# Final norms behind the next block's sets, the last two tiles in two banks, and first biases in three operations

## The chip, the cores and the metric

The kernel runs on one core of a Trainium2 chip. The metric is the device time of one execution in microseconds (us). The time before is 3287.83 us, the median of three runs (3287.54 to 3289.83).

The engines are named as in the profile: PE (matrix products; PEld is its weight load), DVE (vector), ACT (scalar, activations and copies), POOL (the general engine, used here for small per-row values and some subtractions) and SP, whose queue issues all DMAs in program order. Each engine works through its own queue in order; a waiting instruction holds everything behind it.

## What is computed

An attention stage over windows of 128 rows, then a feed-forward stage whose weights are mixed from eight experts for each of the four batches; after each stage a layer norm and a residual. Cut to what matters:

```python
x = x + _layernorm(_L0_attn_ref(_layernorm(x), w_qkv))       # 4 x 2048 x 512
h = relu(x @ gate_w1.T + gate_b1); g = mean over rows (h @ gate_w2.T + gate_b2)
mW1 = W1 + sum_e g[e] * TW1[e];  mb1 = b1 + g @ Tb1
mW2 = W2 + sum_e g[e] * TW2[e];  mb2 = b2 + g @ Tb2
u = gelu(x @ mW1.T + mb1)                                    # 2048 wide
x = x + _layernorm(u @ mW2.T + mb2)
```

All in float32. The last line's layer norm and sum are the "final norms" below. `mb1` are the "first biases".

## The kernel before

**Two phases.** The attention phase runs over 256 slots (64 windows of four groups); next to the scores, exponentials, transposes and values, it carries the projections, the gate's products and, from slot 84, the mixer. The mixer is a generator (`mixer`, steps called with `next(blend)`): each step loads an expert's tile of 512 KB three steps ahead (L119) and adds one on DVE (L144, 128x1024); after eight of them a ninth step makes sums (L152 to L155) and stores the mixed weights to DRAM. The order of instructions is written out by hand; the program doesn't reorder.

**First biases.** When a batch's gate is done, `gate_end` gives four functions. `experts` brings g into SBUF; `first_biases` (L216) adds the eight experts' biases to b1, one SCALAR_TENSOR_TENSOR for each expert (L219), every one on the result of the one before. It is called once per batch: three times in the attention phase, and for the last batch in the feed-forward phase, behind product 5 of block 0.

**The feed-forward phase** runs over 16 blocks of 512 rows (K = 0 to 15; four per batch). A block has two halves.

The first half is four sets (c = 0, 2, 4, 6). Each set makes seven products by a Winograd-like scheme on 256x256 quarters. `begin(n)` issues X (A11), a copy of X into bank Y on ACT (L851), Z (S1) and a copy of it (L853). `middle(n, ...)` issues Y (A12), X (S2), a copy cpb of X (L865), then `end` of the set before (product A22 into that set's X, six gelus on ACT, and `more_sums`: two subtractions on POOL, L889 and L890), two gelus of its own, Z (S4), the add cpb on DVE (L871), X (S3) and the add cpv on DVE (L874). Between them stand steps of the mixer, four per set in most blocks, two per set in block 0 and in the last block of a batch. The first set of a block has no `end` in it; the last set's `end` is issued inside product 0 of the second half (`closing`), after the first four of sixteen products.

The second half (`second`) is seven products of 256 columns (L912, `product2`), each followed by adds into the tiles y0 (tiles 0 and 1 of 128 rows) and y1 (tiles 2 and 3) on DVE (L931). Its weights come through three buffers, `load_second` loading three products ahead. Product 5 completes y1, product 6 completes y0.

**The final norm of a tile** has these parts: `stats` (L85: statistics and aggregate on DVE, then the sum with EPS, L92, and the power, L94, on POOL), `standard` (L987: the shift on POOL, L990, then scale and shift on ACT in place, L991), and `finish` (L993: the residual tile x1 plus y on DVE, L996, and the store, L997). `load_x1` (L983) loads a residual tile from DRAM; the tag "x1" has two buffers, so a third load waits until the first one's store has left.

In a block the order is: tiles 2 and 3 in product 6 (`stats`, `standard`, then the add of c21, then `finish`); `stats` of tiles 0 and 1; their residuals are loaded; the two wait in the list `pending`. In sets 0 and 1 of the next block one each is taken: `standard` behind `begin`, `finish` behind `middle`. For the last block they come at the end of the program.

Of the kernel before, what the change touches and what calls it, by code (L numbers as in the profile page):

```python
# [9 lines left out]
F32 = mybir.dt.float32  # L10
AF = mybir.ActivationFunctionType
ALU = mybir.AluOpType
AX = mybir.AxisListType
# [3 lines left out]
P = 128  # L17
# [9 lines left out]
NX = 8  # L27
# [7 lines left out]
def sandwich(ctx: ExitStack, tc: tile.TileContext, x, w_qkv, gw1, gb1, gw2, gb2, w1, b1, w2, b2, tw1, tb1, tw2, tb2, out):  # L35
# [159 lines left out]
    def gate_end(b, hsum, bank, spare):  # L195

        hm = small.tile([P, KC], F32, tag="hm", name=f"hm_{b}")
        parts = small.tile([P, KC, NX], F32, tag="parts", bufs=1, name=f"parts_{b}")
        part = small.tile([P, NX], F32, tag="part", bufs=1, name=f"part_{b}")
        gc = small.tile([NX, 1], F32, tag="gc", name=f"gc_{b}")  # L200

        def means():

            nc.vector.tensor_reduce(hm, hsum, AX.X, ALU.add)
            nc.vector.tensor_tensor(parts, gw2_sb, hm.unsqueeze(2).to_broadcast([P, KC, NX]), ALU.mult)
            nc.vector.tensor_reduce(part, parts.rearrange("p k e -> p e k"), AX.X, ALU.add)

        def experts():
            pg = bank(f"pg_{b}")
            nc.tensor.matmul(pg[:, :NX], lhsT=ones, rhs=part, start=True, stop=True)  # L210
            nc.tensor.matmul(pg[:NX, NX : NX + 1], lhsT=part, rhs=ones[:, :1], start=True, stop=True)
            nc.vector.scalar_tensor_tensor(gc, pg[:NX, NX : NX + 1], 1.0 / L, gb2_col, ALU.mult, ALU.add)
            nc.vector.scalar_tensor_tensor(g_all[b], pg[:, :NX], 1.0 / L, gb2_row, ALU.mult, ALU.add)
            nc.vector.tensor_copy(gcb[:NX, :], gc.to_broadcast([NX, P]))

        def first_biases():  # L216
            mb1 = mb1_all[b]
            for e in range(NX):
                nc.vector.scalar_tensor_tensor(  # L219
                    mb1, tb1_sb[:, e, :], g_all[b][:, e : e + 1], b1_sb if e == 0 else mb1, ALU.mult, ALU.add  # L220
                )

        def second_biases():
            pb = bank(f"pb_{b}")
            nc.tensor.matmul(pb, lhsT=gcb, rhs=tb2_sb, start=True, stop=True)
            mb2 = spare(f"mb2s_{b}")
            nc.vector.tensor_copy(mb2, pb)
            nc.sync.dma_start(mb2_d[b], mb2)

        return means, experts, first_biases, second_biases  # L230
# [563 lines left out]
    with ExitStack() as fctx:  # L794
# [107 lines left out]
                w2s[g] = wts.tile([P, HC, Q], F32, tag="w2s", bufs=3, name=f"w2s_{g}")  # L902
                nc.sync.dma_start(w2s[g], m2_d[K // NBLK][:, order[j]])

        def product2(K, j, bank, right, start, closing=None):

            w = w2s.pop(7 * K + j)
            for c in range(HC):
                if c == 2 and closing:
                    end(*closing)  # L910
                for t in range(2):
                    nc.tensor.matmul(  # L912
                        bank[:, t, :],
                        lhsT=right(c - c % 2)[:, c % 2, ts(t, P)],
                        rhs=w[:, c, :],
                        start=(start and c == t == 0),
                        stop=True,
                        skip_group_check=True,
                    )
            load_second(7 * K + j + 3)  # L920
# [4 lines left out]
        def second(K, closing, steps, load_x1):  # L925

            mb = mb2_of[K // NBLK]
            mlo, mhi = (mb[:, i * Q : (i + 1) * Q].unsqueeze(1).to_broadcast([P, 2, Q]) for i in range(2))
            y = {h: io.tile([P, 2, D], F32, tag=f"y{h}", bufs=1, name=f"y{h}_{K}") for h in range(2)}
            (c11, c21), (c12, c22) = ((y[h][:, :, :Q], y[h][:, :, Q:]) for h in range(2))  # L930
            add = lambda out, bank, other: nc.vector.tensor_tensor(out, bank, other, ALU.add)  # L931
            b11 = lambda c: us[c][:, :, :Q]
            t3 = lambda c: us[c][:, :, Q:]
            b21 = lambda c: us[c + HC][:, :, :Q]
            b22 = lambda c: us[c + HC][:, :, Q:]
            t1 = lambda c: t1s[c]
            X, Z, Y = bank2("x2", f"px2_{K}"), bank2("z2", f"pz2_{K}"), bank2("y2", f"py2_{K}")

            product2(K, 0, X, b11, True, closing)
            steps()  # L940
            add(c11, X, mlo)
            yield
            product2(K, 1, Z, t1, True)
            steps()
            add(c22, Z, mhi)
            yield
            product2(K, 2, Y, b21, True)
            for c in range(0, HC, 2):
                nc.gpsimd.tensor_tensor(t1s[c], b22(c), t1s[c], ALU.subtract)
            steps()  # L950
            add(c11, Y, c11)
            yield
            product2(K, 3, X, t1, False)
            for c in range(0, HC, 2):
                nc.gpsimd.tensor_tensor(b21(c), b21(c), t1s[c], ALU.subtract)
            steps()
            add(c12, X, mlo)
            yield
            product2(K, 4, Z, b22, False)
            steps()  # L960
            add(c12, Z, c12)
            load_x1(K, 2)
            load_x1(K, 3)
            yield
            product2(K, 5, X, t3, False)
            steps()
            add(c21, X, mhi)
            add(c22, X, c22)
            yield
            Y = bank2("y2", f"py2b_{K}")  # L970
            product2(K, 6, Y, b21, True)
            for t in range(2):
                standard(K, t + 2, y[1][:, t, :], stats(y[1][:, t, :], f"d{K}_{t + 2}"))
            steps()
            add(c21, Y, c21)
            for t in range(2):
                finish(K, t + 2, y[1][:, t, :])
            for t in range(2):
                pending.append((K, t, y[0][:, t, :], stats(y[0][:, t, :], f"d{K}_{t}")))
                load_x1(K, t)  # L980
            yield

        def load_x1(K, t):  # L983
            x1s[K, t] = io.tile([P, D], F32, tag="x1", name=f"fx1_{K}_{t}")
            nc.sync.dma_start(x1s[K, t], x1_d[K * WB + t])

        def standard(K, t, y, sm):  # L987
            mv, rs = sm
            shift = small.tile([P, 1], F32, tag="shift", name=f"shift_{K}_{t}")
            nc.gpsimd.tensor_scalar(shift, mv[:, 0:1], rs, -1.0, ALU.mult, ALU.mult)  # L990
            nc.scalar.activation(y, y, AF.Identity, bias=shift, scale=rs)  # L991
# [57 lines left out]
        nc.sync.dma_start(win[last]["x"], x[NB - 1, L - P :])  # L1049
        for g in range(3):  # L1050
            load_second(g)
        pending = []

        def mixing(*counts):

# [8 lines left out]
        for K in range(NBK):  # L1064
            b, k = divmod(K, NBLK)
            if k == 0:
                mb2_of[b] = io.tile([P, D], F32, tag="mb2", bufs=1, name=f"mb2_{b}")
                nc.sync.dma_start(mb2_of[b], mb2_d[b])
            before = None
            for c in range(0, HC, 2):  # L1070
                n = K * (HC // 2) + c // 2
                if n == 0:

                    for cc in (0, HC):
                        for f in range(2):
                            bias = mb1_all[0][:, cc + f : cc + f + 1]
                            nc.scalar.activation(us[cc][:, f, :], us[cc][:, f, :], AF.Gelu_apprx_tanh, bias=bias)
                    more_sums(0, 0)
                    for f in hooks[("set", 0)]:
                        f()  # L1080
                    continue
                S = begin(n)
                if pending:
                    standard(*pending[0])

                if n < 2:
                    step = mixing(0, 0, 0, 0)
                elif K == 0 or (k == NBLK - 1 and b + 1 < NB):
                    step = mixing(0, 1, 0, 1)
                else:  # L1090
                    step = mixing(1, 1, 1, 1)
                middle(n, S, before, step)
                before = (n, S)
                if pending:
                    finish(*pending.pop(0)[:3])
                for f in hooks.get(("set", n), ()):
                    f()
            for j, _ in enumerate(second(K, before, mixing(2, 2, 2, 2, 2, 2, 1), load_x1)):

                if j == (0 if K else 3) and K + 1 < NBK:  # L1100
                    load_block(K + 1)
                if j == (2 if K else 5) and K + 1 < NBK:
                    right_sums(K + 1)
                for f in hooks.get(("product", K, j), ()):
                    f()
        for p in pending:
            standard(*p)
            finish(*p[:3])


# [54 lines left out]
```

## Time and profile before

| | us |
|---|---|
| median of three runs (lowest, highest) | 3287.83 (3287.54, 3289.83) |
| the profiled execution | 3289.09 |
| its span, first to last instruction | 3287.3 |
| PE busy (share of the span) | 3257.1 (99%) |
| DVE busy | 2072.9 (63%) |
| ACT busy | 1573.1 (48%) |
| POOL busy | 720.8 (22%) |
| mean granted clock of PE, share of full speed | 0.996 |

The profile is of one execution. Its span is what the timeline shows; the execution's own time is 1.8 us longer. The attention phase ends at about 1722 us of the span, the feed-forward phase fills the rest; the last matmul ends at 3276.57.

"Idle before, <- releaser" in a line is the time in which the engine stood before that instruction, and the instruction that released it. In the chain of waits each line is a piece of the work that ended last, followed back from the end. Idle time of an engine other than PE costs nothing unless PE waits for it in turn.

### The profile page before, as it was taken

The page shows a single profiled execution, that of the slowest core. Times are in us where ns is not written, and L with a number is a line of the kernel's source. Part 1 is how long each engine was busy: PE and PEld are TensorE (multiplying, and loading weights), DVE is VectorE, ACT ScalarE, POOL GpSimd, SP SyncE. Part 2 cuts the span into 40 slices and gives each one's busy share as a digit, 9 for nine tenths or more (in the row PEclk, how much of TensorE's full clock was granted, in tenths as well). Part 3 has the DMA queues.
Part 4 walks back from the last instruction along what each step waited for, and adds up shares of the span by engine and source line. Part 5 has one row for each costly group of instructions (what it writes and reads, how often), then busy time and mean ns, then how long its engine had stood idle before and what let it go on. Part 6 is the DMA issues. An engine that isn't in the chain of part 4 may idle for free.

```text
span 3287.3 us, 58445 instructions
## 1 busy us (share of the span) xinstructions
PE 3257.1 (99%) x22830; PEld 2624.7 (80%) x22830; DVE 2072.9 (63%) x2887; ACT 1573.1 (48%) x4212; POOL 720.8 (22%) x841
## 2 busy tenths in 40 slices
PE   9999999999999999999999999999999999999998
PEld 7777777777777777777768888888888888888887
DVE  5656555888888888888884665565556656412221
ACT  3777767777776777767772221212222122222121
POOL 1111110122221122111113322332322333321222
PEclk9999999999999999999999999999999999999999
DMA  2111111556665566656777788988788888732332
GB/s 85 49 59 53 43 52 53 169 193 203 215 211 184 193 201 215 195 178 198 237 255 270 266 293 324 327 294 296 274 322 323 302 288 305 278 107 90 128 128 77
DMA packets 316118, 651.96 MB, mean 198 GB/s; under 512 B 22969, under 2 KB 89657, under 8 KB 295490
## 3 DMA queue, kind: packets, MB, share of 16 engines
q1 hardware_dynamic: 315842, 648.22, 56.9%
q8 instruction: 180, 2.95, 0.4%
q14 instruction: 96, 0.79, 0.1%
HBM read 538.03 MB, written 110.10 MB: 197 GB/s over the span
## 4 chain that ended last, share of the span: by engine, by line
PE 95%; DVE 1%; DMA 1%; ACT 1%; POOL 1%; issue 0%; SPq 0%; DVEq 0%; POOLq 0%; ACTq 0%
PE pm L443 18%; PE px L814 13%; PE ptp L547 10%; PE px L912 9%; PE sc L510 7%; PE pz L912 7%; PE pz L814 6%; PE pmg L163 6%; PE po L563 6%; PE py L912 3%; PE py L814 3%; PE py2b L912 3%; DMA exps<-in_tw 1%; PE pto L240 1%; PE ptx L269 1%; PE pt_a L363 1%
## 5 line engine op out<-in xcount | busy, mean ns | idle before, releaser
L144 DVE SCALAR_TENSOR_TENSOR acc<-exps,g,acc 128x1024 f32<-128x1024 f32 x512 | 685.2, 1338 | 183.0 <-DMA exps<-in_tw 176.7
L532 ACT ACTIVATE pr<-sc,nm 128x384 f32<-128x384 f32 (+1 forms) x1024 | 574.9, 582 | 211.2 <-DVE nm L519 211.1
L519 DVE TENSOR_REDUCE nm<-sc 128x2 f32<-128x768 f32 (+1 forms) x512 | 449.6, 918 | 281.8 <-PE sc L510 280.0
L549 ACT COPY prT<-ptp 128x512 f32<-128x512 f32 x736 | 385.8, 593 | 165.9 <-PE ptp L547 160.9
L991 ACT ACTIVATE y<-y,shift,rs_d 128x512 f32<-128x512 f32 x64 | 52.0, 813 | 739.1 <-POOL shift L990 739.1
L547 PEld LDWEIGHTS ptp<-ident,pr 128*128 128x128 f32 x2944 | 330.0, 141 | 54.5 <-issue 33.8
L547 PE MATMUL ptp<-ident,pr 128*128 128x128 f32 x2944 | 372.8, 276 | 0.0
L814 PE MATMUL px<-tT,w 128*128 128x256 f32 x1512 | 349.9, 379 | 1.9 <-ACT cpb L865 1.9
L814 PEld LDWEIGHTS px<-tT,w 128*128 128x128 f32 x1512 | 286.7, 190 | 42.3 <-ACT cpb L865 3.3
L510 PE MATMUL sc<-k,q 32*128 32x384 f32 (+2 forms) x2816 | 243.5, 423 | 5.6 <-ACT pr L532 5.4
L871 DVE TENSOR_TENSOR cpb<-pz,cpb 128x512 f32<-128x512 f32 x63 | 43.5, 690 | 325.0 <-PE pz L814 278.2
L92 POOL TENSOR_SCALAR ve_b<-mv_b 128x1 f32<-128x1 f32 x64 | 47.1, 736 | 841.5 <-DVE mv_b L90 841.5
L912 PE MATMUL px<-w2s,u 128*128 128x256 f32 x1024 | 228.9, 379 | 0.7 <-ACT last L274 0.7
L532 ACT ACTIVATION_READ_ACCUMULATOR pr<-sc,nm 128x1 f32 x1024 | 224.0, 219 | 0.0
L912 PEld LDWEIGHTS px<-w2s,u 128*128 128x128 f32 x1024 | 194.5, 190 | 27.3 <-ACT last L274 0.9
L163 PE MATMUL pmg<-gT,gw_sb 128*128 128x512 f32 x480 | 215.9, 592 | 0.0
L563 PE MATMUL po<-prT,v 128*32 128x128 f32 x5888 | 214.6, 277 | 0.1
L563 PEld LDWEIGHTS po<-prT,v 128*32 128x32 f32 x5888 | 145.2, 109 | 71.7 <-issue 56.8
L889 POOL TENSOR_TENSOR t<-u 128x512 f32<-128x512 f32 x64 | 84.0, 1313 | 504.6 <-ACT u L826 488.8
L443 PE MATMUL pm<-xnT,wqkv 128*128 128x256 f32 x744 | 183.8, 390 | 0.0
L443 PEld LDWEIGHTS pm<-xnT,wqkv 128*128 128x128 f32 x744 | 135.1, 191 | 41.6 <-ACT oT L570 22.7
L510 PEld LDWEIGHTS sc<-k,q 32*128 32x128 f32 x2816 | 119.1, 184 | 61.2 <-issue 45.9
(168 smaller groups left out, 5301.4 us busy)
## 6 DMA issues: line engine op xcount, KB each, us to landing
exps<-in_tw SPq DMA_DIRECT2D x512, 512.0 KB, 5.8
w2s<-m2d SPq DMA_DIRECT2D x112, 1024.0 KB, 6.1
acc<-in_w SPq DMA_DIRECT2D x64, 512.0 KB, 6.4
x<-in_x SPq DMA_DIRECT2D x64, 256.0 KB, 3.0
m1d<-acc SPq DMA_DIRECT2D x64, 256.0 KB, 6.0
m2d<-acc SPq DMA_DIRECT2D x64, 256.0 KB, 6.6
w<-m1d SPq DMA_DIRECT2D x16, 1024.0 KB, 8.0
fxT<-xTd SPq DMA_DIRECT2D x16, 1024.0 KB, 8.7
```

The source lines that it names most:

```text
L144: nc.vector.scalar_tensor_tensor(acc, ets.pop(n), g_all[b][:, e : e + 1], acc, ALU.mult, ALU.add)
L163: nc.tensor.matmul(pm, lhsT=gw1_sb[:, kc, ts(oc, P)], rhs=xT[:, kc, :], start=(kc == 0), stop=(kc == KC - 1))
L443: nc.tensor.matmul(bank[key][:, half, :], lhsT=a[:, kc, ts(half, P)], rhs=b[:, kc, :], start=(begins and half == kc == 0), stop=True, skip ...
L510: nc.tensor.matmul(scs[r // 2][:, r % 2, col : col + nj * W], lhsT=q[rows, g, ts(W_ % WB, W)], rhs=k_of[kb][rows, g, j0 * W : (j0 + nj) * ...
L519: nc.vector.tensor_reduce(st["nm"][:, h : h + 2], scs[u][:, :, : nk * W], AX.X, ALU.max, negate=True)
L532: nc.scalar.activation(pr[:, : nk * W], scs[r // 2][:, r % 2, : nk * W], AF.Exp, bias=st["nm"][:, h : h + 1], accum_out=st["den"][:, h : h ...
L547: nc.tensor.transpose(pt[:, r, :], st["pr"][g * 4 + r][:, ts(j, W)], ident)
L549: nc.scalar.copy(prT, pt)
L563: nc.tensor.matmul(po[r * E : (r + 1) * E, 0, :], lhsT=v_of[kb][:, jj, h * E : (h + 1) * E], rhs=prT[:, r, :], start=(j == 0), stop=(j == ...
L814: nc.tensor.matmul(bank[:, f, :], lhsT=factor[:, f, kc * P : (kc + 1) * P], rhs=right[:, kc, :], start=(start and f == 0 and kc == 0), sto ...
L889: nc.gpsimd.tensor_tensor(t1s[c], b12, us[c][:, :, :Q], ALU.subtract)
L912: nc.tensor.matmul(bank[:, t, :], lhsT=right(c - c % 2)[:, c % 2, ts(t, P)], rhs=w[:, c, :], start=(start and c == t == 0), stop=True, ski ...
```

## The change

Three parts.

1. `first_biases`: one product of all eight experts' biases with g (128x128), one sum over the experts (128x128 to 128x16), and one add of b1.
2. In all blocks but the last, tiles 2 and 3 join the list `pending` in product 6 instead of being finished there, and tiles 0 and 1 follow. Behind each set of the next block, first the tiles normed behind the set before are finished (`normed_y`), then, if these were tiles 2 and 3, the residuals of tiles 0 and 1 are loaded, then up to two more tiles get their `standard`. So tiles 2 and 3 are normed behind set 0 and finished behind set 1; tiles 0 and 1 are normed behind set 1 and finished behind set 2.
3. In the last block the residuals of tiles 0 and 1 are loaded after product 4 into buffers of the tag "cp". Product 6 runs tile by tile: tile 0 into bank y2, tile 1 into bank z2. Statistics of the finished half of each tile are taken ahead; then each tile is added, its second half measured, both halves aggregated, normalised on DVE (`normalize`, L97) and finished on its own.

```diff
         def first_biases():
             mb1 = mb1_all[b]
-            for e in range(NX):
-                nc.vector.scalar_tensor_tensor(
-                    mb1, tb1_sb[:, e, :], g_all[b][:, e : e + 1], b1_sb if e == 0 else mb1, ALU.mult, ALU.add
-                )
+            weighted = small.tile([P, NX, FC], F32, tag="weighted", bufs=1, name=f"weighted_{b}")
+            nc.vector.tensor_tensor(weighted, tb1_sb, g_all[b].unsqueeze(2).to_broadcast([P, NX, FC]), ALU.mult)
+            nc.vector.tensor_reduce(mb1, weighted.rearrange("p e c -> p c e"), AX.X, ALU.add)
+            nc.vector.tensor_tensor(mb1, mb1, b1_sb, ALU.add)
...
-        def product2(K, j, bank, right, start, closing=None):
-            w = w2s.pop(7 * K + j)
+        def product2(K, j, bank, right, start, closing=None, tiles=range(2)):
+            w = w2s[7 * K + j]
             for c in range(HC):
                 if c == 2 and closing:
                     end(*closing)
-                for t in range(2):
+                for t in tiles:
...
             load_x1(K, 2)
             load_x1(K, 3)
+            if K + 1 == NBK:
+                for t in range(2):
+                    load_x1(K, t, "cp", 4)
...
             Y = bank2("y2", f"py2b_{K}")
-            product2(K, 6, Y, b21, True)
+            if K + 1 < NBK:
+                product2(K, 6, Y, b21, True)
+                for t in range(2):
+                    pending.append((K, t + 2, y[1][:, t, :], stats(y[1][:, t, :], f"d{K}_{t + 2}")))
+                steps()
+                add(c21, Y, c21)
+                for t in range(2):
+                    pending.append((K, t, y[0][:, t, :], stats(y[0][:, t, :], f"d{K}_{t}")))
+                yield
+                return
+
+            Z = bank2("z2", f"pz2b_{K}")
+            product2(K, 6, Y, b21, True, tiles=(0,))
+            product2(K, 6, Z, b21, True, tiles=(1,))
             for t in range(2):
                 standard(K, t + 2, y[1][:, t, :], stats(y[1][:, t, :], f"d{K}_{t + 2}"))
-            steps()
-            add(c21, Y, c21)
+            halves = [small.tile([P, 2, 6], F32, tag="halves", bufs=2, name=f"halves_{t}") for t in range(2)]
+            for t in range(2):
+                nc.vector.bn_stats(halves[t][:, 0, :], c11[:, t])
+            def summed(t, bank):
+                nc.vector.tensor_tensor(c21[:, t], bank[:, t, :], c21[:, t], ALU.add)
+                nc.vector.bn_stats(halves[t][:, 1, :], c21[:, t])
+                mv = small.tile([P, 2], F32, tag="mv", name=f"mv_e{t}")
+                nc.vector.bn_aggr(mv, halves[t])
+                rs = small.tile([P, 1], F32, tag="rs", name=f"rs_e{t}")
+                nc.gpsimd.tensor_scalar(rs, mv[:, 1:2], EPS, None, ALU.add)
+                nc.gpsimd.tensor_tensor(rs, rs, mhalf, ALU.pow)
+                return mv, rs
+
+            sm = summed(0, Y)
             for t in range(2):
                 finish(K, t + 2, y[1][:, t, :])
-            for t in range(2):
-                pending.append((K, t, y[0][:, t, :], stats(y[0][:, t, :], f"d{K}_{t}")))
-                load_x1(K, t)
+            normalize(y[0][:, 0, :], y[0][:, 0, :], sm)
+            sm = summed(1, Z)
+            finish(K, 0, y[0][:, 0, :])
+            normalize(y[0][:, 1, :], y[0][:, 1, :], sm)
+            finish(K, 1, y[0][:, 1, :])
...
                 S = begin(n)
-                if pending:
-                    standard(*pending[0])
...
                 middle(n, S, before, step)
                 before = (n, S)
-                if pending:
-                    finish(*pending.pop(0)[:3])
+
+                for p in normed_y:
+                    finish(*p)
+                for p in normed_y:
+                    if p[1] >= 2:
+                        load_x1(p[0], p[1] - 2)
+                normed_y.clear()
+                for p in pending[:2]:
+                    standard(*p)
+                    normed_y.append(p[:3])
+                del pending[:2]
...
-        for p in pending:
-            standard(*p)
-            finish(*p[:3])
```

## The prediction, as it was put on record

> **What bounds the kernel now.** First the page's share of busy time, then what TensorE (PE) waited for, then the places of those waits in order of time, last the chain that ends the span.
>
> ```profile
> PE 3257.1 (99%) x22830; PEld 2624.7 (80%) x22830; DVE 2072.9 (63%) x2887; ACT 1573.1 (48%) x4212; POOL 720.8 (22%) x841
> ```
>
> PE is the bound: 30.2 us of 3287.3 are without a matmul. The change leaves every matmul in place (the two-bank form issues the same 32 records), so it can win only from these 30 us. The waits of PE (total, times, longest):
>
> ```profile
> PE pm L443 <- DVE q L461: 4.8, 3, 2.5
> PE py L814 <- ACT py L851: 3.8, 3, 2.3
> PE px L814 <- ACT cpb L865: 1.9, 3, 1.1
> ```
>
> The last two rows lie behind three of the 15 block ends (blocks 0, 3 and 7): stalls of 2.26 and 1.06, 0.56 and 0.41, 0.98 and 0.42 us, together 5.69. One of them in the timeline (start, duration, engine, line; in brackets the idle time before and what ended it):
>
> ```profile
> 2114.32 1.89 PE L814 MATMUL pz<-tT,w 128*128 128x256 f32 x8
> ...
> 2115.43 0.81 ACT L991 ACTIVATE y<-y,shift,rs_d 128x512 f32<-128x512 f32 x1 [0.89 <-POOL shift L990]
> 2116.15 0.58 ACT L851 COPY py<-px 128x512 f32<-128x512 f32 x1
> 2116.78 1.99 PE L814 MATMUL py<-fxT,w 128*128 128x256 f32 x8 [0.56 <-ACT py L851]
> ...
> 2122.64 1.99 PE L814 MATMUL px<-tT,w 128*128 128x256 f32 x8 [0.41 <-ACT cpb L865]
> ```
>
> The reader is to see the order on ACT: the norm of tile 3 (L991) sits ahead of the copy py that PE needs, and waits for its shift. The second stall is the same with tile 0's norm ahead of the copy cpb (ACT had waited 4.07 us for that shift). At the other 12 block ends the same waits fit into PE's slack.
>
> In the attention phase two DVE-bound stalls stand behind the first biases (timeline of DVE, then of PE):
>
> ```profile
> 1011.02 0.20 DVE L219 SCALAR_TENSOR_TENSOR mb<-tb_sb,g,b_sb 128x16 f32<-128x16 f32 x1
> 1011.26 1.86 DVE L219 SCALAR_TENSOR_TENSOR mb<-tb_sb,g,mb 128x16 f32<-128x16 f32 x7
> 1013.03 0.54 DVE L99 TENSOR_SCALAR x<-x,mv_c,rs_c 128x512 f32<-128x512 f32 x1
> ```
> ```profile
> 1018.47 1.99 PE L443 MATMUL pm<-xnT,wsum 128*128 128x256 f32 x8 [2.11 <-DVE q L461]
> ```
>
> From 1010.20 to 1018.42 DVE has no gap, and PE's operands (scores, pm) were ready by 1014.9. The same queue ends in a 2.50 us stall at 1437.8. The first-bias groups at 591 and 1816 have none behind them that they cause: at 591 DVE is idle 1.77 us soon after; at 1816 the stall belongs to ACT.
>
> The end of the chain (start, length, what):
>
> ```profile
> 3269.65 6.92 PE py2b L912 x32
> ...
> 3277.20 0.69 DVE fx L996
> 3277.89 0.02 issue
> 3277.91 2.06 DMA out<-fx
> 3279.97 0.02 issue
> 3279.99 2.75 DMA fx<-x1d
> ```
>
> After the last matmul (3276.57) 10.73 us pass: the residual of tiles 0 and 1 is loaded only when the stores of tiles 2 and 3 have left their buffers, and only then added.
>
> **Part 1: norms of a block moved behind the next block's sets.** At the end of a block ACT loses the norms of tiles 2 and 3, and the two others no longer stand ahead of cpb. ACT is then idle when X (A11) is complete, copies at once, and the six stalls go: -5.69 us. Where do the norms land? A set lasts 7 products of 1.73 us = 12.1, the first 6 = 10.4. In set 0 they follow the two gelus behind cpb: cpb at 6.9 after the set's start, gelus to 8.4, two norms at 0.81 to 10.0, while the next copy py is due at 12.1. Without ACT's and the adds' delays the last statistics end at 1823.8 at the latest block end (block 0, set start 1817.4), 2 us ahead of the norms. Cost nothing; the cover is 2.1 us. In set 1 the shifts of tiles 0 and 1 queue on POOL behind the two subtractions of set 0 (L889, L890, median 1.27 each). Measured from the next copy py these start at -5.5; undisturbed they end at -2.9, the shift at -2.6, two norms at -1.0: nothing. PE starts the product that needs the copy at +1.47, the copy takes 0.57, so ACT may be 0.9 late before PE waits.
>
> DVE: the same four adds (0.68 each), now two behind set 1 and two behind set 2 instead of two in product 6 and one in each of sets 0 and 1; four steps of the mixer (1.28), two adds (0.69) and these fill 7.9 of 12.1 us.
>
> SP: four stores and two loads per block move. The two loads wait until the stores have landed, and hold the mixer's loads queued behind them:
>
> ```profile
> 2309.01 0.95 SPq L997 DMA_DIRECT2D out<-fx  x2
> 2317.59 0.97 SPq L985 DMA_DIRECT2D fx<-x1d  x2
> 2318.61 1.45 SPq L119 DMA_DIRECT2D exps<-in_tw  x3
> ```
> ```profile
> 2323.75 1.28 DVE L144 SCALAR_TENSOR_TENSOR acc<-exps,g,acc 128x1024 f32<-128x1024 f32 x1 [4.85 <-DMA exps<-in_tw]
> ```
>
> Today that pause of 9.60 us from store to next expert load, plus 5.14 until the weights are there, hits set 1. After the change it starts about 2.9 us into set 2; three prefetched tiles are used, and the fourth step waits. With pause + landing = S, DVE has worked off that step, two adds, two steps, the cpb add, a step and the cpv add (7.9 us) at 2.9 + S - 12.1 + 7.9 = S - 1.3 after the start of set 3. The closing product A22 (in product 0 of the second half) needs cpv at 12.1 + 1.73 = 13.8. So PE waits from S = 15.1. The block shown has 14.7; with the mean wait for a store (84.8 us over 32, two per block: 5.3), issues of 1.6 and the median landing of 6.9 in this phase, S is 13.8. Value taken: 0.5 us in all over the eight blocks with four steps per set (blocks 1, 2, 4, 5, 6, 8, 9, 10); bounds 0 and, at the longest store wait of the profile (8.5, pause 10.5) and the longest landing (11.8), 8 x 7.2 = 58.
>
> **Part 2: last two tiles one by one.** Tile 0's bank is complete 3.46 us before the last matmul, at 3273.11. DVE until then: adds to 3270.98, statistics of tiles 2 and 3 to 3272.85, two half statistics. A 128x256 BATCH_NORM_STATS is not in the trace: between 0.18 (six elements) and 0.69 (512); I take 0.42, since an add goes from 0.69 to 0.43 at half size. So DVE reaches tile 0's add at 3273.6 and its mean and variance at 3274.7. The adds of tiles 2 and 3 follow their norms (ACT ends 3274.17 and 3275.50) to 3276.2, tile 0's normalisation (L99's kind, 0.53) to 3276.7. Then tile 1: add 0.43 to 3277.05, half statistics from 3277.1, and by today's spacing at 3278.40 (aggregate 0.1 behind the end, POOL 0.27 after it starts, pow 0.31 later for 0.57) the scale is there 1.57 us after the half statistics start: 3278.7. Normalise 0.53, add 0.68: 3280.0. Today the last add ends at 3284.21 and the span at 3287.3, so 3.1 follow: 3283.1. The residuals are loaded some 14 us ahead into free cp buffers. Gain 4.15 us; three ops of half size, each off by up to 0.27, make it 3.3 to 4.9.
>
> **Part 3: first biases.** Eight dependent operations take 2.01 us (1011.02 to 1013.03). New: a 128x128 product, between 0.19 (128x32, L205) and 0.43 (128x256), by size 0.29; a reduction of 128 elements, between 0.21 (32, L206) and 0.92 (768, L519), by size 0.30; an add of 16, 0.14 to 0.19, taken 0.18; with 0.02 between them 0.83. Saved 1.18 (0.41 to 1.41) per group, and it counts at the two stalls, since everything behind was ready: -2.36 us (-0.8 to -2.8). The groups at 591 and 1816 save nothing.
>
> **Sum.** -5.69 - 4.15 - 2.36 + 0.5 = -11.7 us. The profiled execution took 3289.09 us, its span 3287.3 and 1.8 around it; it lies 1.26 above the median of the runs shown, 3287.83. From the median: 3276.1 us.
>
> **Rivals.** *The clock adds to the gain.* Right behind the 2.50 us stall the granted clock is 0.50 from 1440.7 to 1444.1; behind the 2.11 us stall it is not. If the shorter stall (1.3 us) no longer trips it, 3.4 us at half speed give back 1.7: 3274.4. Against it: the clock halves at 1642.1 too, behind stalls of 0.7 us at most.
> The Trainium skill (TensorE: Matmul & The Clock Gate, "What's actually happening") says the gate watches free-running windows of about 3.4 us and halves after an idle one. The 3.4 us length agrees with the trace; that one is needed idle doesn't, since 2.5 us did it. By its rule no stall here would cost clock, and 3276.1 stands.
>
> *ACT waits for POOL in set 1.* For it: L889 and L890 stretch to 1.79 and 2.14 us, a shift to 1.10, when DVE runs the mixer. All at once: subtractions to -1.5, shifts to +0.7, norms to +1.5, copy to +2.1 where 1.45 is the limit: 0.65 in each of 15 blocks, +9.8: 3285.9. Against: at that point of set 1 DVE no longer catches up, so it mostly adds out of PSUM.
> The Trainium skill (GPSIMD Engine Reference, "1. Specifications") says GpSimd shares its SBUF interfaces with VectorE and meets contention from instructions with two SBUF inputs. The mixer step has two, and 2.14 against 1.27 agrees; where they always met, this rival's time would follow.
>
> *DVE takes ACT's place.* The stalls come after a late DVE (at 2104 and 2108 it waited 3.12 and 2.60 us for expert weights); if its adds then hold PE at the same block ends, the 5.69 return: 3281.8. Against: nothing PE needs in the next set's first 8 us comes from DVE but tT, ready 3 us early at 1816.0.
>
> *SP's pause, the other side.* S above 17.4 in the eight blocks makes 8 x 2.3 = 18.7 us and the kernel slower by over 0.2%; at S = 18.5, 8 x 3.4 = 27: 3303. For: store waits of 8.5 and landings of 11.8 occur. Against: the store there queued behind a 1 MB w2s load, which set 2 doesn't have.
>
> **Chances.** 0.2% (6.6 us) is about what a measurement of this kernel tells from no change: faster means below 3281.25. Forecast 0.60, clock 0.14, POOL 0.08, DVE 0.11, SP 0.07. Faster 0.74, same 0.19, slower 0.07. Range 3273 to 3283: the clock case with the biases' upper bound below, the DVE case with a short tail gain above, 0.85 of the chances; those left out are POOL and SP.
>
> **What would show it.** Right: no waits of PE on ACT's py or cpb at block ends; stalls near 0.9 and 1.3 us at 1016 and 1437; 6.6 us from last matmul to the end. Wrong: ACT idle for POOL's shift in set 1 with PE behind it, or PE's A22 of set 3 waiting for cpv on DVE.

## The result, and the profile after

The changed kernel takes 3272.25 us in the median of six runs (3270.06 to 3274.05); the kernel before, beside it, 3288.83 (3285.61 to 3290.95). The ratio is 0.9951, 95% interval 0.994 to 0.9961: about 16.6 us or 0.5% faster. The forecast was 11.7 us; the measured time lies 0.75 us below the stated range. The profiled execution took 3270.06 us, its span is 3268.3, so in the two profiles the spans differ by 19.0.

| | before | after |
|---|---|---|
| span of the profiled execution, us | 3287.3 | 3268.3 |
| block-end waits of PE on py and cpb, us | 5.7 | none |
| attention stalls, us | 2.11 and 2.50 | 0.88 and 1.27 |
| last matmul to the end, us | 10.7 | 6.8 |
| mean granted clock | 0.996 | 0.999 |

Page of the changed kernel, shares of busy time:

```profile
PE 3249.4 (99%) x22830; PEld 2620.8 (80%) x22830; DVE 2062.9 (63%) x2872; ACT 1569.7 (48%) x4210; POOL 718.9 (22%) x839
```

PE has the same 22830 records and is busy 7.7 us less. Waiting was not all that went: the same matmuls took less time, which points to the clock. What PE still waits for (total, times, longest):

```profile
PE sc L510 <- ACT pr L532: 5.9, 14, 1.0
PE pm L443 <- DVE q L461: 2.3, 3, 1.3
```

The rows with py and cpb are gone, and the longest wait for q is halved. The end of block 3 and the sets behind it, in order of time (start, duration, engine, line):

```profile
2102.70 1.89 PE L814 MATMUL pz<-tT,w 128*128 128x256 f32 x8
...
2102.96 0.57 ACT L851 COPY py<-px 128x512 f32<-128x512 f32 x1 [47.56 <-PE px L814]
...
2104.43 1.89 PE L814 MATMUL py<-fxT,w 128*128 128x256 f32 x8
...
2108.08 0.58 ACT L865 COPY cpb<-px 128x512 f32<-128x512 f32 x1 [2.87 <-PE px L814]
...
2109.29 1.52 ACT L1021 ACTIVATE y<-y,shift,rs_d 128x512 f32<-128x512 f32 x2
```

ACT has idled 47.56 us when PE releases it, and copies at once; PE goes from Z to Y with no gap. The two norms (L1021) come behind the gelus and end at 2110.8, 2.5 us ahead of the next copy.

The first biases of batch 1 on DVE:

```profile
1007.30 0.26 DVE L219 TENSOR_TENSOR weighted<-tb_sb,g 128x128 f32<-128x128 f32 x1
1007.60 0.37 DVE L220 TENSOR_REDUCE mb<-weighted 128x16 f32<-128x128 f32 x1
1008.00 0.18 DVE L221 TENSOR_TENSOR mb<-mb,b_sb 128x16 f32<-128x16 f32 x1
1008.09 0.54 DVE L99 TENSOR_SCALAR x<-x,mv_c,rs_c 128x512 f32<-128x512 f32 x1
```

From the first to the next operation behind them 0.79 us, where the eight took 2.01.

The end. The last matmul is over at 3261.46:

```profile
3261.50 0.42 DVE L994 TENSOR_TENSOR y<-pz2b,y 128x256 f32<-128x256 f32 x1
3261.95 0.43 DVE L995 BATCH_NORM_STATS2 halves<-y 128x6 f32<-128x256 f32 x1
3262.41 0.21 DVE L997 BATCH_NORM_AGGREGATE mv_e<-halves 128x2 f32<-128x12 f32 x1
3262.54 0.64 DVE L1026 TENSOR_TENSOR fx<-fx,y 128x512 f32<-128x512 f32 x1
3262.71 0.54 POOL L999 TENSOR_SCALAR rs_e<-mv_e 128x1 f32<-128x1 f32 x1 [1.89 <-DVE mv_e L997]
3263.34 0.57 POOL L1000 TENSOR_TENSOR rs_e<-rs_e,mhalf 128x1 f32<-128x1 f32 x1
3263.94 0.55 DVE L99 TENSOR_SCALAR y<-y,mv_e,rs_e 128x512 f32<-128x512 f32 x1 [0.77 <-POOL rs_e L1000]
3264.52 0.69 DVE L1026 TENSOR_TENSOR fx<-fx,y 128x512 f32<-128x512 f32 x1
```

No load of a residual lies in this chain any more. The one row that differs from the working is L999: 0.54 us, against 0.23 for the same step before, while DVE adds tile 0's residual; that is why 6.8 us remain and not 6.6.

**Where the 19.0 us of the two spans lie.** The order and number of matmuls are the same, so the n-th matmul of one profile can be set against the n-th of the other; the difference of their start times grows at a few places only:

```
stretch of the kernel before            after minus before, us
0 to 160     (clock halved before, full after)     -3.9
160 to 1010                                        +0.2
the stall at 1016                                  -1.2
the stall at 1437                                  -2.9   (1.2 stall, 1.7 clock)
ends of blocks 0, 3, 7               -3.8, -1.5, -1.9     (-7.3 together)
last matmul to the end                             -3.9
```

The block ends gave 7.3 us and not the 5.7 that the six gaps show. One gap shows why. Before, the eight products of pz started at 2114.32 and those of py at 2116.78: 2.46 us. After, 2102.70 to 2104.43: 1.73. The difference is 0.73 for a gap shown as 0.56, since the gap starts at the modelled end of a matmul and the next one normally starts 0.16 before it. The first group after the gap also took 0.1 longer to start the one behind it. About 0.27 us more per stall, 1.6 for six.

The rest is the clock. Of the stretches where it was halved in the kernel before (near 55, 143, 1441 and 1642 us) one was left, the last. The first two lie in code that the change doesn't touch, the third behind the shortened stall. That third place, before and then after (stretch in us, its length, busy time of PE, PEld, DVE, ACT and POOL with their instructions, then PE's granted clock, DMA share and GB/s):

```profile
1440.72:1444.13 3.41, 3.41 (x16) 2.30 (x18) 2.80 (x4) 1.95 (x6) 0.00 (x0) 0.50 0.71 217
```
```profile
1434.30:1438.00 3.70, 3.70 (x42) 2.47 (x43) 3.50 (x5) 2.48 (x8) 0.00 (x0) 1.00 0.77 252
```

Whether that is chance is what the experiments had to tell.

### The profile page after: what moved, and what is told of

Read it like the earlier page. It is cut to its first block, busy times and chain, and to the rows that moved or that the text cites. A ratio compares the mean times of both kernels' runs of the same rounds, so it can differ in the third digit from the quotient of the medians.

```text
span 3268.3 us, 58364 instructions
## 1 busy us (share of the span) xinstructions
PE 3249.4 (99%) x22830; PEld 2620.8 (80%) x22830; DVE 2062.9 (63%) x2872; ACT 1569.7 (48%) x4210; POOL 718.9 (22%) x839
## 4 chain that ended last, share of the span: by engine, by line
PE 97%; DVE 1%; ACT 1%; issue 0%; DMA 0%; POOL 0%; POOLq 0%; SPq 0%; ACTq 0%; DVEq 0%
PE pm L443 18%; PE px L814 13%; PE px L912 10%; PE ptp L547 10%; PE pz L912 7%; PE pz L814 7%; PE sc L510 7%; PE pmg L163 6%; PE po L563 6%; PE py L912 3%; PE py L814 3%; PE py2b L912 3%; PE pto L240 1%; PE ptx L269 1%; PE pt_a L363 1%; ACT pr L532 1%
## 5 line engine op out<-in xcount | busy, mean ns | idle before, releaser
L851 ACT COPY py<-px 128x512 f32<-128x512 f32 x63 | 35.9, 570 | 803.7 <-PE px L814 803.7
```

## The experiments

All differences below are medians against the kernel before on the same chip, with the ratio's 95% interval. First each part by itself, and the kernel before against itself.

**The norms alone**

```diff
+            if K + 1 < NBK:
+                product2(K, 6, Y, b21, True)
+                for t in range(2):
+                    pending.append((K, t + 2, y[1][:, t, :], stats(y[1][:, t, :], f"d{K}_{t + 2}")))
...
-                if pending:
-                    standard(*pending[0])
...
+                for p in pending[:2]:
+                    standard(*p)
+                    normed_y.append(p[:3])
```

> Part 1 alone: the norms of blocks 0 to 14 behind the next block's sets; first biases and the last block's end as before. Theory (stalls): the six block-end stalls go, 5.7 us off, so about 5.7 below the kernel before; in the profile no wait of PE on ACT's py or cpb, the two attention stalls stay at 2.1 and 2.5 us, the end from last matmul stays 10.7. Rival (the surplus of 4.5 us comes from the clock behind the block-end stalls): about 10 below, and the profile of a kernel with these stalls would show halved clock behind them. Rival (the surplus is chance in where the clock halves): 5.7 below in the median, and the profile's span after taking off half of each halved stretch is 5.7 below the one of before taken likewise.

Measured: 3281.41, 7.2 below before (0.9965 to 0.9985). Its waits of PE have no row of py or cpb; the first two are:

```profile
PE sc L510 <- ACT pr L532: 5.2, 13, 1.0
PE pm L443 <- DVE q L461: 4.8, 3, 2.5
```

Set against the profile of before, matmul by matmul, the three block ends gave 3.8, 1.5 and 1.9 us again: 7.3, as much as the median. Against the 5.7 us of the gaps that is 1.6 more. The surplus over the forecast as a whole (16.6 measured, 11.7 forecast) does not sit here. But this profile has something that the one before lacks, a halved clock behind both attention stalls (columns as above):

```profile
1018.09:1021.50 3.41, 3.41 (x35) 1.92 (x34) 2.44 (x4) 1.29 (x5) 0.00 (x0) 0.50 0.97 335
1441.34:1444.75 3.41, 3.41 (x32) 2.17 (x35) 2.34 (x3) 1.47 (x6) 0.00 (x0) 0.50 0.64 219
```

**The tail alone**

```diff
+            if K + 1 == NBK:
+                for t in range(2):
+                    load_x1(K, t, "cp", 4)
...
+            product2(K, 6, Y, b21, True, tiles=(0,))
+            product2(K, 6, Z, b21, True, tiles=(1,))
```

> Part 2 alone: the last block's tiles one by one in two banks. All theories: the end from the last matmul shrinks from 10.7 to 6.8 us, 3.9 off; the clock has no part in it, so a median further than 2 us from that says how much the runs scatter.

Measured: 3284.69, 4.0 below (0.9977 to 0.9994); in its profile 7.3 us from the last matmul to the end, where 6.8 were expected. The median is as expected. Its 2.3 us stall at the end of block 0 is followed by a halved stretch, 1823.2 to 1826.6, which the two profiles of the unchanged kernel don't have at that place.

**The first biases alone**

```diff
-            for e in range(NX):
...
+            nc.vector.tensor_reduce(mb1, weighted.rearrange("p e c -> p c e"), AX.X, ALU.add)
+            nc.vector.tensor_tensor(mb1, mb1, b1_sb, ALU.add)
```

> Part 3 alone: first biases in three operations. Theory (stalls only): the two attention stalls shrink to 0.9 and 1.3 us, 2.5 off. Rival (the clock no longer halves behind the 1437 us stall): 4.2 off, and no halved stretch near 1440 us in the profile.

Measured: 3282.40, 6.2 below (0.9971 to 0.9989). The attention stalls are 0.88 and 1.27 us, which gives 2.4. A third stall shrank too: the 2.26 us one at the end of block 0, where the last batch's first biases stand on DVE ahead of the statistics that the norms, and with them the copy py, wait for. Before, then here:

```profile
1823.30 1.99 PE L814 MATMUL py<-fxT,w 128*128 128x256 f32 x8 [2.26 <-ACT py L851]
```
```profile
1815.28 1.99 PE L814 MATMUL py<-fxT,w 128*128 128x256 f32 x8 [0.81 <-ACT py L851]
```

Matmul by matmul that place gave 1.4 us. The remaining 2.4 are no stall, and the profile has no halved stretch behind any of the three. In the whole change part 1 removes the third stall anyway, so the two parts can't both win it.

**The kernel before against itself**

> The kernel before, unchanged, against itself. 0 in the median if the runs of this kind separate by less than 1 us; its profile is a second sample of where the clock halves: theory (chance) has the halved stretches near 55 and 143 us in other places or absent, and the one near 1440 back if the stall of 2.5 us causes it.

Measured: 3289.75, 1.1 above (0.9993 to 1.0011), so medians of this kind separate only to a microsecond or two. In its profile the clock is halved near 55, 1437 and 1639 us but not near 143: the stretch behind the 2.5 us stall is there again, the one at 143 comes and goes.

The clock shows in the runs without a profile as well. Of 55 runs of the kernel before, by mean granted clock, the 18 at 0.996 took 3290.4 us on average, the 25 at 0.997 took 3288.8, and the 11 at 0.998 took 3286.4 (one at 0.995 took 3293.5).

**The rule behind it.** Between the first 8 us and the last matmul, the halved stretches of every profile last 3.41 us or twice that, and start a whole number of 3.413 us apart (to within 0.02 us), so they sit on a grid that runs through the kernel. Laid over the attention and block-end stalls, this grid tells in all profiles taken so far whether the next stretch is halved:

```
idle PE inside one 3.41 us stretch   next stretch
2.07, 2.10, 2.27, 2.49, 2.49, 2.50   halved
1.98                                 full
1.55, 1.41, 1.28, 1.27 and less      full
```

The table doesn't hold in the score code near 55, 143 and 1640 us: there the clock halved behind stretches with 0.85 to 1.36 us of idle. At these stalls, one of 2.1 us costs its length or 1.7 us more, by where it falls on the grid; none of 1.3 us did. The average is an estimate: with a threshold of 2.05 us (between 1.98 and 2.07), and all positions on the grid equally likely, a stall of g us is followed by a halved stretch in a share (3.41 + g - 4.1) / 3.41 of cases: 0.42, 0.53 and 0.46 for the stalls of 2.11, 2.50 and 2.26 us, worth 2.4 us together. Two experiments try this.

**Longer stalls**

```diff
+            for _ in range(2):
             for e in range(NX):
```

> The kernel before with the eight first-bias operations of each batch made twice (the second time over the first). The two attention stalls should grow by 2.0 us each, to 4.1 and 4.5. Theory (a free-running stretch of 3.41 us with more than about 2.0 us of PE idle halves the clock of the next one; of the stalls so far those with 2.1 us or more inside one stretch did, those with 1.97 or less did not): now some stretch always holds more than 2 us of idle, so the profile shows halved stretches behind both stalls, and the median rises by 4.0 for the work and by 1.7 us times the share of runs in which the shorter stalls were spared (about half each): 5.0 to 6.5 above before. Rival (where the clock halves has nothing to do with these stalls): 4.0 above before.

Measured: 3301.80, 13.2 above (1.0031 to 1.0058). More than either theory. The work was counted wrongly: all four batches' biases lie on the path once they are long enough. The profile has a new stall of 1.8 us at 593, 4.3 and 4.7 in place of 2.1 and 2.5, and at the end of block 0 4.1 in place of 2.3, so the work is 8 us and not 4. The remaining 5 are put down to the clock: the five runs' mean granted clock is 0.995 on average, against 0.997 for the kernel before. In the profile, behind each of the three long stalls the clock is halved, once for two stretches (columns as above):

```profile
1019.31:1022.72 3.41, 3.41 (x27) 2.32 (x29) 3.18 (x6) 1.71 (x6) 0.00 (x0) 0.50 0.95 330
1442.56:1449.38 6.82, 5.03 (x32) 3.52 (x32) 5.36 (x7) 3.82 (x11) 0.00 (x0) 0.50 0.84 290
1828.27:1831.68 3.41, 3.00 (x7) 2.46 (x8) 3.34 (x6) 0.88 (x2) 1.82 (x3) 0.50 0.53 180
```

They held 2.79, 2.89 and 3.41 us of idle in one stretch. After the second, the next stretch had 1.79 and stayed halved (one case), so a stretch that is itself halved seems to need less.

**Stalls under the threshold**

```diff
-            for e in range(NX):
+            for e in range(5):
```

> The kernel before with the first biases of five experts only (three are left out of the sum). The two stalls shrink by three operations, 0.75 us, to about 1.35 and 1.75, below 2.0. Theory (threshold near 2.0 us): no halved stretch behind them, 1.5 off for the stalls and 1.5 to 1.7 more for the clock, 3.0 to 3.2 below before, as much as 70% of what part 3 alone gained beyond... its 2.4 us of stall. Rival (the clock follows the stall's length smoothly): a halved stretch behind the 1.75 us stall still appears. Rival (chance): 1.5 below before.

The kernel leaves out the biases of three experts. Measured: 3284.58, 4.1 below (0.9979 to 0.9997). The stalls are 1.30 and 1.69 us; on the grid no stretch holds more than 1.39 us of their idle time. No halved clock behind either of them:

```profile
1017.00:1024.00 7.00, 6.21 (x60) 4.81 (x61) 6.83 (x13) 5.28 (x14) 0.00 (x0) 1.00 0.89 284
1437.00:1444.00 7.00, 5.31 (x56) 3.84 (x55) 6.80 (x9) 4.93 (x14) 0.00 (x0) 1.00 0.79 279
```

The two stalls gave 1.6 of the 4.1 us, though most of each is still there; the third, at the end of block 0, went from 2.26 to 1.36 us and gave 0.9, which was not in the expectation. Matmul by matmul the place at 1437 gave 2.4 us, 0.8 of stall and 1.6 of clock, as the threshold has it and against a smooth dependence on the length. The interval of the time alone (1.0 to 6.9 us) would not exclude chance; here the profile decides. It doesn't say where between 1.39 and 2.07 us the threshold lies: the bound from below is the one case of 1.98.

**Parts 1 and 2 together, without part 3**

The diff is against the changed kernel.

```diff
-            nc.vector.tensor_reduce(mb1, weighted.rearrange("p e c -> p c e"), AX.X, ALU.add)
-            nc.vector.tensor_tensor(mb1, mb1, b1_sb, ALU.add)
...
+            for e in range(NX):
```

> The changed kernel with the first biases as before (parts 1 and 2 alone). Theory (the parts add up, part 3 being worth 2.4 of stall and about 1.7 to 2 of clock): about 4.3 above the changed kernel, 3276.5 where that has 3272.2; block-end waits still gone, attention stalls 2.1 and 2.5 us. Rival (part 3 is worth its stalls alone): 2.4 above. Rival (the 6.2 us of part 3 alone are all real): 6.2 above.

Measured: 3276.53, 12.1 below before (0.9954 to 0.9979) and 4.3 above the changed kernel's 3272.25. The parts add up, and part 3 is worth 4.3 in this company: 2.4 of stall and 1.9 of clock. The 6.2 of part 3 alone are more because the stall at the end of block 0 was still there to be shortened: 2.4 and 1.4 of stall, and an estimated 2.4 of clock behind three stalls, make 6.2.

**First biases where nobody waits**, again against the changed kernel

```diff
-                rest[s0 + KC + 2].append(first_biases)
+                if b == 0:
+                    rest[s0 + KC + 2].append(first_biases)
+                else:
+                    deferred.append(first_biases)
...
-            ("product", 0, 0): [load_gate_last],
+            ("product", 0, 0): [load_gate_last, deferred[0]],
+            ("product", 0, 1): [deferred[1]],
```

> The changed kernel with the first biases of batches 1 and 2 made in the feed-forward phase, behind products 0 and 1 of block 0, where DVE has room; they are needed only from block 4 on. The three operations take 0.8 us on DVE ahead of the stalls: these should shrink from 0.9 to about 0.1 and from 1.3 to about 0.5 us, nothing new waits. 1.6 us below the changed kernel, about 3270.6; no clock term, since no stall of 2 us is left there. Rival (what is behind on DVE waits for expert weights instead): no change.

Measured: 3270.52, 18.1 below (0.9936 to 0.9961). Waits of PE for q in this kernel:

```profile
PE pm L443 <- DVE q L461: 0.6, 2, 0.5
```

The two stalls are all but gone. Because its distance to the changed kernel (1.7) is near the scatter, both ran again side by side, with a third that defers the eight operations of before.

> The changed kernel once more, beside the two below on the same chip. About 16.5 below before again (3272). Threshold theory: no halved stretch behind its two attention stalls of 0.9 and 1.3 us.

> The changed kernel with the first biases of batches 1 and 2 in the feed-forward phase, once more: both attention stalls gone (they were 0.9 and 1.3 us), 1.5 to 2.2 below the changed kernel. If the earlier difference of 1.7 was scatter, the medians lie within 1 us.

> Deferred likewise, but with the eight operations per batch of before. Theory (only the place ahead of the two stalls mattered, not the number of operations): within 1 us of the three deferred operations, no attention stall. Rival (the shorter form helps elsewhere as well, at 591 us or at the end of block 0): 1 to 2 us longer.

Measured, against 3289.95 for the kernel before: the changed kernel 3271.61 (0.9934 to 0.9959), deferred 3270.61 (0.9929 to 0.9954), deferred with eight operations 3269.86 (0.9926 to 0.9953). The first difference is 1.0, below the 1.5 to 2.2 that was expected and inside the scatter, so the median doesn't tell it from none. The profile does: matmul by matmul the attention stalls gave 2.0 us at 1016 and 3.7 at 1437 (clock included) against 1.2 and 2.9 in the changed kernel. The eight operations in the new place cost nothing that shows: the place was the matter, not their number. The deferred kernels are below the changed one by 1 to 2 us in each of three comparisons of medians, none of which exceeds the scatter alone.

## Why the prediction was right in kind and too small

**Part 1.** Right in mechanism: the six block-end stalls went, alone and together. Its term was mis-sized: 5.69 was read from the gaps, 7.3 came off, since each stall costs some 0.27 us beyond its gap.

**ACT behind POOL.** The rival did not decide. ACT waited for the shifts 22 times, 56.8 us in all, and no matmul waited for py or cpb. POOL's second subtraction still took 2.13 us at worst, but the slack of 0.9 us was never used up.

**SP's pause.** The term of +0.5 us was too much: the pause did not just move, it shrank. Queue of DMA issues around the new place in block 4, then the total wait of residual loads for stores (it was 84.8 us, 32 times, longest 8.5):

```profile
2126.27 0.96 SPq L1027 DMA_DIRECT2D out<-fx  x2
...
2129.34 2.16 SPq L119 DMA_DIRECT2D exps<-in_tw  x3
```
```profile
SPq L1015 <- DMA out<-fx: 24.5, 30, 3.3
```

Here 3.1 us pass from store to the next expert load; behind the stores that the prediction showed with 9.6 it is 5.3 now. The traces fit what was said against the rival (no 1 MB load ahead of the stores in that place), which should then have stood in the sum; no run tries it alone. PE's waits show no A22 on cpv. (In the rival of the longer pause 8 x 2.3 is 18.4, not 18.7.)

**Part 2.** 3.9 us against 4.15; the half-size statistics took 0.43 (taken: 0.42). The difference is POOL's step of 0.54.

**Part 3.** 0.79 us for the three operations (taken: 0.83); the stalls shrank by 1.23 each (taken: 1.18). One reading failed without harm: the group at 1816 was said to save nothing, the stall there being ACT's. ACT's wait began with DVE, and part 3 alone took 1.4 us off it; in the sum part 1 already had that stall.

**The step that failed** is the clock, kept out of the sum and put down as a rival with a chance of 0.14. The reason given against it (the clock halves at 1642 as well, behind shorter stalls) mixed two things: a second place that halves with 0.9 us of idle in the stretch ahead, for a reason that stays open, doesn't clear the stall at 1437. The granted clock stood halved right behind the 2.50 us stall in the profile shown, and in all four later profiles with a stall of that length (part 1 alone, part 2 alone, the kernel before again, parts 1 and 2). It belonged in the sum, as an average of 1.7 us times the share of positions, 2.4 us over the three long stalls. With it, 7.3 + 3.9 + 2.4 + 2.4 = 16.0 off, and 16.6 was measured; the 0.6 between them is inside the scatter. Next to it the largest mis-sized term is part 1's: of the 4.9 us beyond the forecast the clock is an estimated 2.4, the stalls' part beyond their gaps 1.6, SP's term 0.5. The lower end of the range took the clock case once, behind one stall, and part 1 at 5.69, so it stopped at 3273.

What stays open: in the two profiles 3.9 us more went in the first 160 us, in code that the change leaves alone. Halved stretches came and went there between profiles of kernels that don't differ in it, so this is counted as chance between two profiles. The other way, two of the three long stalls had no halved stretch behind them in the profile before. The medians differ by 16.6 and not by 19.0. Why the clock halves there and near 1640, behind gaps of 1.0 us and less, was not tried.

## What to carry to other kernels

On a bound engine a stall costs more than the gap that the profile draws: here 0.27 us each, and half a stretch of 3.41 us when more than about 2 us of idle time fall into one stretch. Between the two profiles, shortening the 2.50 us stall by 1.2 won 2.9. An in-order engine that does a late, dependent piece ahead of an early copy is cured by moving the piece one stage on, where its inputs are old; look then at the queues it is moved past, as they can get better as well (here the loads' total wait for stores fell from 84.8 to 24.5 us). And a small operation in front of a stall is best moved to a place where nobody waits: here eight instructions there cost no more than three, within the scatter.

## What the runs showed of the hardware

The granted clock of PE fell to 0.50 for one stretch of 3.41 us after a stretch of the same grid with 2.07 us or more of idle PE (ten cases, at the attention and block-end stalls), and stayed at full there with 1.98 us or less (a stretch that was itself halved, with 1.79 us, kept it halved). In the score code near 55, 143 and 1640 us it fell behind 0.85 to 1.36 us. The Trainium skill (TensorE: Matmul & The Clock Gate, "What's actually happening") has the free-running 3.4 us stretch, which agrees; it asks for an idle one, where 2.07 of 3.41 us was enough here.

POOL's addition of EPS took 0.54 us in place of 0.23 while DVE added two tensors from SBUF (two cases, both in the tail of the changed kernel); beside a DVE addition with one operand from PSUM it took 0.23.
